# Channel-major images and residual, contexts formed from x itself, probabilities normalised on GpSimd, and values held stationary in the last product

## The chip, the cores and the metric

The kernel runs on one core of one Trainium2 chip. The metric is device microseconds (us) of one execution; each version is run several times and compared by its median. A core has a matrix engine (PE, TensorE; its weight loads are listed apart as PEld), a vector engine (DVE), a scalar engine (ACT), a general one (POOL, GpSimd), and a sync engine (SP) which in this kernel issues all data transfers (DMA). Matrix products are written into PSUM, from which DVE and ACT take them into SBUF.

## The reference

The input x is 16 images of 64 x 64 pixels with 256 channels, all in f32. Two layers follow one another, each as x = x + layer(group_norm(x)), where the norm has 32 groups of 8 channels and averages over the image. Cut to what matters:

```python
def layer0(x):                       # linear attention, 8 heads of 32
    q, k, v = split(x @ w_qkv)       # each (b, head, 32, 4096 tokens)
    q = softmax(q, over the 32 features) * SCALE
    k = softmax(k, over the 4096 tokens)
    context = einsum('bhdn,bhen->bhde', k, v)
    out = einsum('bhde,bhdn->bhen', context, q)
    return out @ w_out

def layer1(x):                       # local attention, 8 heads of 32, 7 x 7 window
    q, k, v = x @ Wq + bq, x @ Wk + bk, x @ Wv + bv
    kp = unfold(k, 7) + e            # 49 keys a query; e: embedding of row or column offset
    attn = softmax(einsum('bhwnd,bhwndk->bhwnk', q, kp))
    return einsum('bhwndk,bhwnk->bhwnd', unfold(v, 7), attn)

x = x + layer0(group_norm(x))
x = x + layer1(group_norm(x))
```

## The kernel before

Sixteen images are worked on one after the other. An image lies in 8 strips (`NS`) of 8 rows, 512 tokens each. The host hands x over in blocks of 8 x 8 pixels, and a strip in SBUF is a tile `xs` of 128 partitions by four times 256 channels: tokens lie on the partitions, two blocks to a column of tokens, four such columns (`t`) to a strip. The `xs` tiles are the residual: both layers add into them, and they are stored from there.

**Layer 0** (`layer0`, from L257) has these stages.

- The head. Every strip is transposed on PE (tile `xt`, 8 transposes a strip, L265) and evacuated by `evac`, which alternates between ACT (L80) and DVE (L82), into `xT`: channels on the partitions, 4096 tokens along them, two halves of 128 channels. `bn_stats` (L269) gathers the statistics. `group_norm` averages them over the groups with two small products (`pm`, L239, and `pv`), takes the reciprocal root on GpSimd (L251) and normalises `xT` in place, 8 operations of 128 x 1024 on DVE (L255).
- Keys. For two groups (`hg`) of four heads and 8 strips, `pk` (L280) is copied by ACT to `kT`, whose row maximum and exponentials over the tokens follow; `rz` is the reciprocal of their sum, times SCALE.
- Contexts. For each group and strip, four transposes of `kT` and eight value products (both in `pkv`, L313 and L317) are evacuated, and four products of 128 columns add to `pc` (L327) over all strips. The four heads' diagonal blocks go to `ctx_bd` (L336), which times w_out gives `pw` (L338) and, scaled by `rz`, `w2` (L339).
- Query strips. `queries` (L348 to L366) makes `pq`, its maximum, difference (L360), exponentials, sums and reciprocals, and a multiplication on GpSimd (L366) gives `qs`. `outputs` transposes `qs` (`pqt`, L373), evacuates it to `qT`, forms `py` (L383: a slice of `qT` stationary, `w2` moving in 256 columns) and adds it to `xs` (L391). `transposed` transposes the sum back to channel-major rows in `xT` (tile `xt` again, L398) with new `bn_stats`. The loop runs queries(s), outputs(s-1), transposed(s-2). The second norm follows.

**Layer 1** begins with `values` (`pv`, L424), whose strips have a bias added and are written to a padded image `vpad` in DRAM. Then for each of two head groups:

- `queries_keys`: `pka` (L454), whose four heads are copied with bias into the padded key tiles `kaug` (ACT L467, DVE L469); then 16 rounds in which GpSimd writes position columns into the query weights (`wqa`, L472, and `comb`, L477) and PE makes queries (`pqa`, L487), which DVE adds into `qa` (L504). In the second group the columns read for a round are 16 apart.
- `local_attention`: each strip has four steps (`t`), a step being two blocks of 64 queries and four heads. `load_window` (L445) fetches the values of a strip's windows, 14 x 14 keys a block, in 14 DMAs one strip ahead, into two buffers (`win`). In `scores`, 8 products (L519) of 196 columns make `s`; DVE takes the negative maxima `nm` (L528); ACT makes four exponentials of 128 x 196 (`p`, L539), and each gives its row sum in `z`. In `weighted`, 8 transposes of `p` (`pt`, L554) are evacuated into `pT`, and 16 products (L560) add to `o`: 64 queries on the partitions by 32 features in the columns, with a slice of `pT` stationary (64 columns) and values moving (32 columns); the two blocks `j` lie in the two halves of the partitions. `finish` takes the reciprocal of 16 sums (L571), multiplies `o` by it into `on` (L573) on DVE, and GpSimd adds `on` to `xs` (L580). In the second group `done` follows: the strip is stored (L602), and when a strip is stored, the previous strip's tile is loaded with the next image (L227).

As written, `weighted` of a step comes after `scores` of the next. A scheduler then orders the instructions of each engine by its own estimate: from the third strip of a group on, PE has the 16 products `o` of four steps together, in one batch a strip.

The buffers: `xs` 8; `work` 6 tiles of 128 x 1024 (p, pT, on, kv, qs, qT, v4 share them); `small` 2 by default; PSUM three pools of 2: `ps2` (s, pq, pkv, pqt, py, xt, pv: two banks each), `ps1` (pk, pka, pqa, pt), `pso` (o, pc, pw and the norm's sums).

Of the kernel before, what the change touches and what calls it, by code (L numbers as in the profile page):

```python
# [10 lines left out]
F32 = mybir.dt.float32  # L11
# [7 lines left out]
W = 64  # L19
C = 256  # L20
HEADS, HD = 8, 32
NS = 8  # strips of 8 image rows
# [3 lines left out]
WIN = 8 + 2 * PAD  # rows and columns of keys that an 8x8 block of queries sees  # L26
NCH = WIN // 2 * WIN  # keys of half a window
# [4 lines left out]
# Columns of the packed constants.  # L32
# [4 lines left out]
def shape_constants():  # L37
    """What depends on shapes alone: group averaging, band selectors and masks."""
# [24 lines left out]
def attention_kernel(ctx: ExitStack, tc: tile.TileContext, x, w_qkv, w_out, wq, bq, wk, bk, wv, bv, emb0, emb1, cpk, onehot, out):  # L63
    nc = tc.nc
    B = x.shape[0]
# [48 lines left out]
    # Keys with their position one-hot: 32 rows of a head, 16 for the row and 16 for the  # L114
    # column (both modulo 16), two heads to a tile. Borders stay zero keys.
# [6 lines left out]
    # Query weights with columns for the positional scores of the current residue.  # L122
# [12 lines left out]
    with tc.tile_pool(name="setup", bufs=1) as sp:  # L135
# [27 lines left out]
        for hg in range(2):  # L163
# [16 lines left out]
            # Scores of a query against the embeddings, as columns of the query weights.  # L180
# [14 lines left out]
            # The same of the query bias, by residue, with the band's mask.  # L195
# [26 lines left out]
    work = ctx.enter_context(tc.tile_pool(name="work", bufs=6))  # L222
    small = ctx.enter_context(tc.tile_pool(name="small", bufs=2))

    def load_strip(b, s):
        t = xp.tile([P, 4, C], F32, tag="xs", name=f"xs{b}_{s}")
        nc.sync.dma_start(t.rearrange("p t c -> p (t c)"), x[b, s])  # L227
        return t

    def group_norm(xT, stats, eps, name):  # L230
        """xT normalised in place, by groups of 8 channels over the image."""
# [20 lines left out]
        for q in range(4):  # L252
            for k in range(2):
                sl = xT[:, k, q * 1024 : (q + 1) * 1024]
                nc.vector.tensor_scalar(sl, sl, mean[:, k : k + 1], rstd[:, k : k + 1], ALU.subtract, ALU.mult)  # L255

    def layer0(b, xs):  # L257
        """x += linear attention of its normalised self; returns the transposed result, normalised."""
        xT = cp.tile([P, 2, NT], F32, tag="xT", name=f"xT{b}")
        st = small.tile([P, 2, NS, 6], F32, tag="st", name=f"st0_{b}")  # L260
        for s in range(NS):
            pt = psum2(f"xt0_{b}_{s}")
            for t in range(4):
                for k in range(2):
                    nc.tensor.transpose(pt[:, k, t * P : (t + 1) * P], xs[s][:, t, k * P : (k + 1) * P], ident)  # L265
            for k in range(2):
                dst = xT[:, k, s * 512 : (s + 1) * 512]
                evac(dst, pt[:, k])
                nc.vector.bn_stats(st[:, k, s], dst)  # L269
        group_norm(xT, st, 1e-5, f"0_{b}")  # L270

        # Keys, exponentiated over the tokens.
        kT, rz = [], []
        for hg in range(2):
            kt = big.tile([P, NT], F32, tag="qk", name=f"kT{b}_{hg}")
            km = small.tile([P, NS], F32, tag="km", name=f"km{b}_{hg}")
            for s in range(NS):
                pk = psum1(f"pk{b}_{hg}_{s}")
                for k in range(2):
                    nc.tensor.matmul(  # L280
                        pk,
                        wqkv_sb[:, k, C + hg * P : C + (hg + 1) * P],
                        xT[:, k, s * 512 : (s + 1) * 512],
                        start=(k == 0),
                        stop=(k == 1),
                    )
# [13 lines left out]
            nc.vector.tensor_scalar(r, r, SCALE, None, ALU.mult)  # L300
# [3 lines left out]
        # Contexts by head, taken through the output weights.  # L304
        w2 = cp.tile([P, 2, C], F32, tag="w2", name=f"w2_{b}")
        for hg in range(2):
            pc = psum_o(f"pc{b}_{hg}")
            for s in range(NS):
                kv = work_tile(f"kv{b}_{hg}_{s}")
                pkv = psum2(f"pkv{b}_{hg}_{s}")  # L310
                for t in range(4):
                    tok = slice(s * 512 + t * P, s * 512 + (t + 1) * P)
                    nc.tensor.transpose(pkv[:, 0, t * P : (t + 1) * P], kT[hg][:, tok], ident)  # L313
                for t in range(4):
                    tok = slice(s * 512 + t * P, s * 512 + (t + 1) * P)
                    for k in range(2):
                        nc.tensor.matmul(  # L317
                            pkv[:, 1, t * P : (t + 1) * P],
                            xT[:, k, tok],
                            wqkv_sb[:, k, 2 * C + hg * P : 2 * C + (hg + 1) * P],  # L320
                            start=(k == 0),
                            stop=(k == 1),
                        )
                evac(kv[:, :512], pkv[:, 0])
                evac(kv[:, 512:], pkv[:, 1])
                for t in range(4):
                    nc.tensor.matmul(  # L327
                        pc[:, :P],
                        kv[:, 512 + t * P : 512 + (t + 1) * P],
                        kv[:, t * P : (t + 1) * P],  # L330
                        start=(s == 0 and t == 0),
                        stop=(s == NS - 1 and t == 3),
                    )
            for h in range(4):
                sl = slice(h * HD, (h + 1) * HD)
                nc.vector.tensor_copy(ctx_bd[hg][sl, sl], pc[sl, sl])  # L336
            pw = psum_o(f"pw{b}_{hg}")
            nc.tensor.matmul(pw[:, :C], ctx_bd[hg], wout_sb[:, hg], start=True, stop=True)  # L338
            nc.vector.tensor_scalar(w2[:, hg], pw[:, :C], rz[hg], None, ALU.mult)  # L339
# [3 lines left out]
        def queries(s):  # L343
            """Softmax of a strip's queries over each head's features, transposed."""
            pq = psum2(f"pq{b}_{s}").rearrange("p a (t c) -> p (a t) c", c=C)
            for t in range(4):
                for k in range(2):
                    nc.tensor.matmul(  # L348
                        pq[:, t],
                        xT[:, k, s * 512 + t * P : s * 512 + (t + 1) * P],  # L350
# [18 lines left out]
        def outputs(s, qs):  # L369
            pt = psum2(f"pqt{b}_{s}")  # L370
            for t in range(4):
                for hg in range(2):
# [7 lines left out]
            py4 = py.rearrange("p a (t c) -> p (a t) c", c=C)  # L380
            for t in range(4):
                for hg in range(2):
                    nc.tensor.matmul(  # L383
                        py4[:, t],
                        qT[:, hg * 512 + t * P : hg * 512 + (t + 1) * P],
                        w2[:, hg],
# [3 lines left out]
            flat = xs[s].rearrange("p t c -> p (t c)")  # L390
            nc.vector.tensor_tensor(flat, py.rearrange("p a c -> p (a c)"), flat, ALU.add)  # L391

        def transposed(s):
            """The strip's sum, transposed from blocks of 8x8 to rows."""
            pt = psum2(f"xt1_{b}_{s}")
            for t in range(4):
                for k in range(2):
                    nc.tensor.transpose(pt[:, k, t * P : (t + 1) * P], xs[s][:, t, k * P : (k + 1) * P], ident)  # L398
            for k in range(2):
                dst = xT[:, k, s * 512 : (s + 1) * 512]  # L400
                evac(
                    dst.rearrange("p (r c w) -> p c r w", r=8, c=8),
                    pt[:, k].rearrange("p (c r w) -> p c r w", r=8, c=8),
                )
                nc.vector.bn_stats(st[:, k, s], dst)

        held = {}
        for s in range(NS + 2):
            if s < NS:
                held[s] = queries(s)  # L410
            if 0 < s <= NS:
                outputs(s - 1, held.pop(s - 1))
            if s > 1:
                transposed(s - 2)
        group_norm(xT, st, 1e-5, f"1_{b}")
        return xT
# [235 lines left out]
```

## Time and profile before

| | |
|---|---|
| time, median of 3 runs | 10178.1 us (10175.57 to 10181.25) |
| span of the profiled execution | 10159.9 us |
| one image of it (16 in a row) | 635 us |
| PE busy | 8906.7 us, 88% |
| PEld busy | 6291.8 us, 62% |
| DVE busy | 4871.0 us, 48% |
| ACT busy | 3437.7 us, 34% |
| POOL busy | 964.1 us, 9% |
| DMA, share of 16 engines, hardware queue | 13.7% |

How to read the profile: a row of it names a source line (L554 is line 554 of the kernel before), an engine, an operation, output <- inputs, the size of one instruction and how often it ran; then busy us in all, mean ns of one, and the idle us of the engine just before such instructions, with what ended most of it ("<-DVE pT" is a DVE operation on tile `pT`). On PE a product in f32 has two instructions, so that counts are twice those in the code. A row of the timeline begins with the time of its start and its length, both in us; `x16` is the number of instructions in it, and the bracket behind it the idle time before it and what ended that. Transposes count as MATMUL with `ident`. PE's ends are modelled, so that starts are surer than lengths. The granted clock of PE is a share of its full rate; in the page's 40 slices it stands at 0.9 or more.

### The profile page before, as it was taken

To read this page: it belongs to the slowest core of one execution; us is meant where nothing else is said; L and a number is where in the kernel's file an instruction comes from. 1 tells how busy PE (TensorE), PEld (TensorE's weight loads), DVE (VectorE), ACT (ScalarE), POOL (GpSimd) and SP (SyncE) were. 2 spreads that over 40 slices of the span, in tenths; PEclk is the share of its full clock that TensorE was granted. 3 is DMA by queue.
4 is the path that set the end of the run, shared out by engine and by line. 5 is a ranking of instruction groups with operands and counts; after the bars stand their busy time and mean duration, and the time that the engine had idled before them with its cause. 6 is when DMAs were issued, how large, how long until landed. Compare 5 with 4: busy or idle time off the path is not lost. (4 is left out here: it accounts for less than half of the span.)

```text
span 10159.9 us, 193328 instructions
## 1 busy us (share of the span) xinstructions
PE 8906.7 (88%) x80084; PEld 6291.8 (62%) x80084; DVE 4871.0 (48%) x7126; ACT 3437.7 (34%) x11009; POOL 964.1 (9%) x1461
## 2 busy tenths in 40 slices
PE   7988989889898898988989889898898988989888
PEld 5666566665666656666565665656656566565665
DVE  4445454454544545445454454544545445444454
ACT  2332423324233242342423424234242342413434
POOL 1101001010010100101001010010100101001010
PEclk9999999999899999999999999999999999999999
DMA  1111101111011110111101111011110111101111
GB/s 43 49 54 31 53 19 49 54 33 53 18 49 54 33 53 18 49 54 33 55 18 47 54 33 59 21 40 54 35 58 20 38 54 36 60 22 34 54 38 48
DMA packets 562853, 425.97 MB, mean 42 GB/s; under 512 B 59548, under 2 KB 528156, under 8 KB 561856
## 3 DMA queue, kind: packets, MB, share of 16 engines
q1 hardware_dynamic: 561984, 413.61, 13.7%
q8 instruction: 640, 10.49, 0.4%
q14 instruction: 229, 1.88, 0.1%
HBM read 277.51 MB, written 135.86 MB: 41 GB/s over the span
## 5 line engine op out<-in xcount | busy, mean ns | idle before, releaser
L539 ACT ACTIVATE p<-s,nm 128x196 f32<-128x196 f32 x4096 | 1679.1, 423 | 2602.2 <-DVE nm L528 2345.5
L554 PE MATMUL pt<-ident,p 128*98 128x128 f32 x8192 | 1455.2, 305 | 319.4 <-DVE pT L82 236.5
L554 PEld LDWEIGHTS pt<-ident,p 128*98 128x98 f32 x8192 | 913.6, 139 | 892.8 <-issue 411.6
L519 PE MATMUL s<-kaug,qa 64*64 64x196 f32 x16384 | 1417.3, 371 | 3.8 <-DVE qa L504 3.8
L487 PE MATMUL pqa<-xT,wqa 128*128 128x256 f32 x4096 | 1353.6, 496 | 44.3 <-DVE qa L504 25.7
L528 DVE TENSOR_REDUCE nm<-s 128x4 f32<-128x784 f32 x1024 | 994.2, 974 | 474.9 <-PE s L519 440.3
L82 DVE COPY pT<-pt 98x512 f32<-98x512 f32 x1024 | 706.1, 690 | 1006.9 <-PE pt L554 961.0
L487 PEld LDWEIGHTS pqa<-xT,wqa 128*128 128x128 f32 x4096 | 783.2, 200 | 613.0 <-issue 415.2
L560 PEld LDWEIGHTS o<-vw,pT 98*64 98x64 f32 x32768 | 1018.7, 138 | 168.3 <-issue 140.7
L560 PE MATMUL o<-vw,pT 98*64 98x32 f32 x32768 | 1094.0, 224 | 7.5 <-ACT pT L80 5.1
L519 PEld LDWEIGHTS s<-kaug,qa 64*64 64x64 f32 x16384 | 691.9, 142 | 411.8 <-issue 323.3
L504 DVE TENSOR_TENSOR qa<-pqa,comb 128x256 f32<-128x256 f32 x1024 | 544.5, 532 | 831.0 <-PE pqa L487 830.5
L539 ACT ACTIVATION_READ_ACCUMULATOR p<-s,nm 128x1 f32 x4096 | 837.7, 205 | 0.0
L383 PE MATMUL py<-w,qT 128*128 128x256 f32 x2048 | 578.4, 443 | 200.0 <-DVE qs L360 172.2
L80 ACT COPY pT<-pt 98x512 f32<-98x512 f32 x1024 | 607.9, 594 | 339.3 <-PE pt L554 305.7
L580 POOL TENSOR_TENSOR xs<-xs,on 128x512 f32<-128x512 f32 x256 | 324.3, 1267 | 4040.4 <-DVE on L573 4040.4
L467 ACT ACTIVATE kaug<-pka,bk_sb 32x512 f32<-32x512 f32 x512 | 351.1, 686 | 1039.6 <-DVE kaug L469 1030.0
L383 PEld LDWEIGHTS py<-w,qT 128*128 128x128 f32 x2048 | 432.4, 221 | 327.7 <-issue 188.2
L454 PE MATMUL pka<-xT,wk_sb 128*128 128x512 f32 x1024 | 497.1, 616 | 118.9 <-ACT kaug L467 118.9
L317 PE MATMUL pkv<-wqkv_sb,xT 128*128 128x128 f32 x4096 | 538.8, 277 | 0.0
L469 DVE TENSOR_SCALAR kaug<-pka,bk_sb 32x512 f32<-32x512 f32 x512 | 379.7, 742 | 284.2 <-ACT kaug L467 180.8
L280 PE MATMUL pk<-xT,wqkv_sb 128*128 128x512 f32 x1024 | 485.1, 635 | 34.1 <-DVE xT L255 30.1
(93 smaller groups left out, 8240.5 us busy)
## 6 DMA issues: line engine op xcount, KB each, us to landing
vw<-vpad SPq DMA_DIRECT2D x3584, 56.0 KB
xs<-in_x SPq DMA_DIRECT2D x128, 512.0 KB
vpad<-v SPq DMA_DIRECT2D x256, 256.0 KB
out<-xs SPq DMA_DIRECT2D x128, 512.0 KB
kaug<-in_shape_onehot SPq DMA_DIRECT2D x4, 612.5 KB
vpad<-zero SPq DMA_DIRECT2D x4, 210.0 KB
wqkv_sb<-in_L_conv_w_qkv SPq DMA_DIRECT2D x1, 768.0 KB
vpad<-zero SPq DMA_DIRECT2D x4, 192.0 KB
```

The lines of the kernel that those rows point to most:

```text
L80: nc.scalar.copy(dst, src)
L82: nc.vector.tensor_copy(dst, src)
L317: nc.tensor.matmul(pkv[:, 1, t * P : (t + 1) * P], xT[:, k, tok], wqkv_sb[:, k, 2 * C + hg * P : 2 * C + (hg + 1) * P], start=(k == 0), st ...
L383: nc.tensor.matmul(py4[:, t], qT[:, hg * 512 + t * P : hg * 512 + (t + 1) * P], w2[:, hg], start=(hg == 0), stop=(hg == 1),)
L454: nc.tensor.matmul(pk, wk_sb[:, k, hg * P : (hg + 1) * P], xT[:, k, s * 512 : (s + 1) * 512], start=(k == 0), stop=(k == 1),)
L487: nc.tensor.matmul(half, wa[:, k, 2 * pl : 2 * pl + 2].rearrange("p a b -> p (a b)"), rows[k][:, r::RING, :] if hg == 0 else rows[k][:, :, ...
L504: nc.vector.tensor_tensor(dst, src, add, ALU.add)
L519: nc.tensor.matmul(ps[64 * j : 64 * j + 64, ab, pl * 2 * NCH : (pl + 1) * 2 * NCH], qa[pl][rows, 8 * s + bc], kaug[pl][rows, 8 * s : 8 * s ...
L528: nc.vector.tensor_reduce(nm, s4, AX.X, ALU.max, negate=True)
L539: nc.scalar.activation(pr[:, h * 2 * NCH : (h + 1) * 2 * NCH], s4[:, ab, pl], AF.Exp, bias=nm[:, ab, pl : pl + 1], accum_out=z[:, t, h : h ...
L554: nc.tensor.transpose(pt[:NCH, h * P : (h + 1) * P], pr[:, n0 : n0 + NCH], ident)
L560: nc.tensor.matmul(o[64 * j : 64 * j + 64, t * P + h * HD : t * P + (h + 1) * HD], pT[:NCH, c * 512 + h * P + 64 * j : c * 512 + h * P + 6 ...
```

## The change

- **Layout.** The host gives x twice: channel-major (`xc`: 128 channels by 2 by 4096 tokens, in row order) and token-major (`xt`). A strip `xs` is now 128 channels by 2 by 512 tokens, and so are the residual and the output; the host transposes the result back.
- **Head and norm.** No transposes: `bn_stats` reads `xs`. The norm writes a separate tile `xn` from `xs` (16 operations of 128 x 512), and returns mean and reciprocal root.
- **Contexts.** The product of the exponentiated keys is formed with x itself, token by channel, 256 columns wide, in place of the values. The token-major halves of a strip are loaded for it (pool `tok`, two buffers of a half-strip). The sum is then scaled by `rz`, the mean subtracted, transposed, scaled by the reciprocal root and multiplied by the value weights. This is a serial sequence between the last context and `w2`; SCALE goes into `w2`.
- **Query strips.** `py` has `w2` stationary and `qT` moving in 512 columns, and comes out channel-major; it is added to `xs` and gets its `bn_stats` there. `transposed` is gone. The second norm goes into `xn1`.
- **Probabilities.** In every step a reciprocal of the four row sums follows the exponentials, and GpSimd multiplies each head's 128 x 196 of `p` by it, in place, before the transposes.
- **Last product.** A slice of the values is stationary (32 columns) and a slice of `pT` moves (64 columns); the four heads lie in four quarters of `o`'s partitions. `finish` is one DVE addition of `o` to `xs`, the columns reordered from blocks to rows.
- **Buffers.** `work` has 5 tiles for 6.

The diff, without comments, the host's side and renamed arguments (xT to xn in products):

```diff
     def load_strip(b, s):
-        t = xp.tile([P, 4, C], F32, tag="xs", name=f"xs{b}_{s}")
-        nc.sync.dma_start(t.rearrange("p t c -> p (t c)"), x[b, s])
+        t = xp.tile([P, 2, 512], F32, tag="xs", name=f"xs{b}_{s}")
+        nc.sync.dma_start(t, xc[b, :, :, s * 512 : (s + 1) * 512])
...
     def group_norm(xs, xn, stats, eps, name):
...
-        for q in range(4):
-            for k in range(2):
-                sl = xT[:, k, q * 1024 : (q + 1) * 1024]
-                nc.vector.tensor_scalar(sl, sl, mean[:, k : k + 1], rstd[:, k : k + 1], ALU.subtract, ALU.mult)
+        for s in range(NS):
+            for k in range(2):
+                nc.vector.tensor_scalar(xn[:, k, s * 512 : (s + 1) * 512], xs[s][:, k],
+                    mean[:, k : k + 1], rstd[:, k : k + 1], ALU.subtract, ALU.mult)
+        return mean, rstd
...
     def layer0(b, xs):
         for s in range(NS):
-            pt = psum2(f"xt0_{b}_{s}")
-            ...
             for k in range(2):
-                evac(dst, pt[:, k])
-                nc.vector.bn_stats(st[:, k, s], dst)
+                nc.vector.bn_stats(st[:, k, s], xs[s][:, k])
+        mean, rstd = group_norm(xs, xn, st, 1e-5, f"0_{b}")
+        pmu = psum_o(f"pmu{b}")
+        for k in range(2):
+            nc.tensor.transpose(pmu[:, k * P : (k + 1) * P], mean[:, k : k + 1].to_broadcast([P, P]), ident)
+        mu = small.tile([P, C], F32, tag="mu", bufs=1, name=f"mu{b}")
+        nc.vector.tensor_copy(mu, pmu[:, :C])
...
-            nc.vector.tensor_scalar(r, r, SCALE, None, ALU.mult)
...
+        pc = [psum_o(f"pc{b}_{hg}") for hg in range(2)]
+        for s in range(NS):
+            xtok = []
+            for i in range(2):
+                xtok.append(tok.tile([P, 2, C], F32, tag="xtok", name=f"xtok{b}_{s}_{i}"))
+                nc.sync.dma_start(xtok[i].rearrange("p t c -> p (t c)"), xt[b, s, :, i * 2 * C : (i + 1) * 2 * C])
+            for hg in range(2):
+                ptk = psum1(f"ptk{b}_{s}_{hg}")
+                for t in range(4):
+                    nc.tensor.transpose(ptk[:, t * P : (t + 1) * P], kT[hg][:, s * 512 + t * P : s * 512 + (t + 1) * P], ident)
+                ek = work_tile(f"ek{b}_{s}_{hg}")[:, :512]
+                evac(ek, ptk)
+                for t in range(4):
+                    nc.tensor.matmul(pc[hg][:, :C], ek[:, t * P : (t + 1) * P], xtok[t // 2][:, t % 2],
+                        start=(s == 0 and t == 0), stop=(s == NS - 1 and t == 3))
+        cc = work_tile(f"cc{b}")[:, : 2 * C].rearrange("p (a c) -> p a c", c=C)
+        pct = psum1(f"pct{b}")
+        for hg in range(2):
+            nc.vector.scalar_tensor_tensor(cc[:, hg], pc[hg][:, :C], rz[hg], mu, ALU.mult, ALU.subtract)
+            for k in range(2):
+                nc.tensor.transpose(pct[:, (2 * k + hg) * P : (2 * k + hg + 1) * P], cc[:, hg, k * P : (k + 1) * P], ident)
+        cT = work_tile(f"cT{b}")[:, :512].rearrange("p (a c) -> p a c", c=P)
+        for k in range(2):
+            dst = cT[:, 2 * k : 2 * k + 2].rearrange("p a b -> p (a b)")
+            nc.vector.tensor_scalar(dst, pct[:, k * C : (k + 1) * C], rstd[:, k : k + 1], None, ALU.mult)
         for hg in range(2):
-            ...
+            px = psum_o(f"px{b}_{hg}")
+            for k in range(2):
+                nc.tensor.matmul(px[:, :P], wqkv_sb[:, k, 2 * C + hg * P : 2 * C + (hg + 1) * P], cT[:, 2 * k + hg], ...)
-                nc.vector.tensor_copy(ctx_bd[hg][sl, sl], pc[sl, sl])
+                nc.vector.tensor_copy(ctx_bd[hg][sl, sl], px[sl, sl])
...
-            nc.vector.tensor_scalar(w2[:, hg], pw[:, :C], rz[hg], None, ALU.mult)
+            nc.vector.tensor_scalar(w2[:, hg], pw[:, :C], SCALE, None, ALU.mult)
...
         def outputs(s, qs):
...
-            for t in range(4):
+            for co in range(2):
                 for hg in range(2):
                     nc.tensor.matmul(
-                        py4[:, t],
-                        qT[:, hg * 512 + t * P : hg * 512 + (t + 1) * P],
-                        w2[:, hg],
+                        py[:, co],
+                        w2[:, hg, co * P : (co + 1) * P],
+                        qT[:, hg * 512 : (hg + 1) * 512],
...
-            nc.vector.tensor_tensor(flat, py.rearrange("p a c -> p (a c)"), flat, ALU.add)
+            nc.vector.tensor_tensor(xs[s], py, xs[s], ALU.add)
+            for k in range(2):
+                nc.vector.bn_stats(st[:, k, s], xs[s][:, k])
-        def transposed(s):
-            ...
...
     def local_attention(b, hg, qa, xs, done):
         def scores(s, t):
...
+            r = small.tile([P, 4], F32, tag="rzz", bufs=3, name=f"rz{b}_{hg}_{s}_{t}")
+            nc.vector.reciprocal(r, z)
+            for h in range(4):
+                sl = pr[:, h * 2 * NCH : (h + 1) * 2 * NCH]
+                nc.gpsimd.tensor_scalar(sl, sl, r[:, h : h + 1], None, ALU.mult)
...
         def weighted(s, t, pr):
...
-            for h in range(4):
+            for j in range(2):
                 for c in range(2):
-                    for j in range(2):
+                    for h in range(4):
                         nc.tensor.matmul(
-                            o[64 * j : 64 * j + 64, t * P + h * HD : t * P + (h + 1) * HD],
+                            o[h * HD : (h + 1) * HD, t * P + 64 * j : t * P + 64 * j + 64],
+                            vw[s][:, c, 2 * t + j, h * HD : (h + 1) * HD],
                             pT[:NCH, c * 512 + h * P + 64 * j : c * 512 + h * P + 64 * j + 64],
-                            vw[s][:, c, 2 * t + j, h * HD : (h + 1) * HD],
...
         def finish(s):
-            z, o = state.pop(s)
-            ...
-            nc.gpsimd.tensor_tensor(dst, dst, on.rearrange("p (t c) -> p t c", t=4), ALU.add)
+            o = state.pop(s)
+            dst = xs[s][:, hg].rearrange("p (r c w) -> p c r w", r=8, c=8)
+            nc.vector.tensor_tensor(dst, o.rearrange("p (c r w) -> p c r w", c=8, r=8), dst, ALU.add)
             done(s)
```

## The prediction

> **What bounds the kernel now.** I read the page's head, then the PE timeline of one image in the middle of the run (5107 to 5735 us), because 16 images pass one after the other and PE holds the order of the work.
>
> ```profile
> span 10159.9 us, 193328 instructions
> PE 8906.7 (88%) x80084; PEld 6291.8 (62%) x80084; DVE 4871.0 (48%) x7126; ACT 3437.7 (34%) x11009; POOL 964.1 (9%) x1461
> L554 PE MATMUL pt<-ident,p 128*98 128x128 f32 x8192 | 1455.2, 305 | 319.4 <-DVE pT L82 236.5
> L560 PE MATMUL o<-vw,pT 98*64 98x32 f32 x32768 | 1094.0, 224 | 7.5 <-ACT pT L80 5.1
> ```
>
> One image takes 10159.9 / 16 = 635 us. PE's 88% does not say that PE is at its peak: its ends are modelled. In layer 0 the waits stand between its groups:
>
> ```profile
> 5107.32 1.97 PE L265 MATMUL xt<-ident,xs 128*128 128x128 f32 x16
> 5115.03 3.85 PE L265 MATMUL xt<-ident,xs 128*128 128x128 f32 x16 [5.75 <-DMA xs<-in_x]
> 5122.31 0.59 PE L239 MATMUL pm<-gn,grp 128*128 128x2 f32 x2 [3.44 <-DVE gn L237]
> 5126.21 19.50 PE L280 MATMUL pk<-xT,wqkv_sb 128*128 128x512 f32 x40 [1.88 <-DVE xT L255]
> 5226.92 1.97 PE L373 MATMUL pqt<-ident,qs 128*128 128x128 f32 x8 [5.96 <-POOL qs L366]
> 5241.02 3.79 PE L383 MATMUL py<-w,qT 128*128 128x256 f32 x16 [1.79 <-DVE qs L360]
> 5244.65 1.04 PE L398 MATMUL xt<-ident,xs 128*128 128x128 f32 x8
> 5246.13 3.72 PE L348 MATMUL pq<-wqkv_sb,xT 128*128 128x256 f32 x16 [0.44 <-DVE xs L391]
> ```
>
> The reader sees the image's head (18.9 us from the last `o` to the first `pk`), and the loop over query strips. In the attention the same strip of four steps repeats:
>
> ```profile
> 5069.03 3.81 PE L560 MATMUL o<-vw,pT 98*64 98x32 f32 x124
> 5074.32 0.61 PE L554 MATMUL pt<-ident,p 128*98 128x128 f32 x4 [1.48 <-DVE pT L82]
> 5075.97 1.58 PE L519 MATMUL s<-kaug,qa 64*64 64x196 f32 x14
> 5079.31 0.91 PE L519 MATMUL s<-kaug,qa 64*64 64x196 f32 x16
> 5086.01 3.81 PE L560 MATMUL o<-vw,pT 98*64 98x32 f32 x124
> ```
>
> `o` of a whole strip is done in one batch, and batch to batch is 16.98 us (5069.03 to 5086.01). Of 14 `s` in 1.58 us and 16 in 0.91 us the first ran at a granted clock of 0.5: after each idle stretch PE is slow for some us. The first two strips of a head group run step by step, 3.12 us each (`o` x32 at 5415.57 and 5418.69).
>
> **Layer 0, part by part.** Head: the transposes of x go, and with them, behind the last load, 3.85 us (16 at low clock) and an evacuation (0.67); the residual add of GpSimd (L580, 1.27 us) in front of the store and the reload goes too. The loads, bn_stats and the norm's chain stay: -5.8 us.
>
> Contexts: from the end of `pk` (5159.5) to the first `py` (5229.6) are 70.1 us. After: 64 transposes of kT at 0.109 us (4 take 0.43) = 7.0; 64 matmuls of 256 columns, each two instructions at 0.216 (`pq`, 16 in 3.45) = 27.6 in place of the value products and narrower contexts; two `pq` groups = 6.9, as before. In the built order they stand among the `pk` and the contexts, so the 5.96 us wait for `qs` goes. New is a serial tail: two scalar_tensor_tensor, transposes, scaling, `px`, four block copies (0.187 each), `pw`, `w2` (0.48), twice in part: some 7 us of such rows and 15 hand-overs of about 0.2 = 10. Then `pqt` and its evacuation, 2.7. The xtok loads have two half-strip buffers: a half is in use for 2.6 of a strip's 4.3 us of PE; a load of 256 KB costs about 2 us (half the bytes of xs, which issues in 0.38 and moves in 1.7), so 4.6 a strip: +2.4. Sum 56.6: -13.5 us.
>
> Queries: the transposes back (1.04) and the 0.44 us wait go out of each of 8 rounds, the `py` columns stay (4 x 512 for 8 x 256); 8 x 1.45 = 11.6, and the norm reads xs where it lies. -11.6 us. Normalising is 16 x 0.54 for 8 x 0.807 us on DVE, behind `pk` and `pv`: 0; uncovered it is +2 a norm.
>
> Layer 0: -30.9 us an image.
>
> **The last product.** Now 128 instructions a strip at 30.7 ns (124 in 3.81 us), two column halves at a time: 61 ns a pair. After, four quarters, each with 32 stationary and 64 moving columns. No row shows this form. `s` has four tiles in turn: 16 of 196 columns in 0.91 us, where one at a time (0.216 / 256 a column) would be 2.65, so four do run together. Lower end: 61 ns for four, 1.96 us a strip, -1.97. Upper end: one at a time, 64 columns at 54 ns, 6.9 us, +3.0. I take the lower end, nearest to `s`.
>
> The Trainium skill, TensorEngine Tiling (Array Packing), Instruction Overhead, gives each matmul about 60 cycles whatever its width and warns against tiling a small dimension; by that (25 ns at its clock) 128 would be an estimated 3.2 us and the gain 0.7. The trace's single starts inside `o` lie 6 to 7 ns apart in a pair and 58 ns from pair to pair, which speaks against a floor per instruction.
>
> **GpSimd's multiplies.** New on every step: reciprocal of 4 (about 0.2), then four 128x196 multiplies, and `pt` waits for all. Nothing else is queued on GpSimd there, but PE's later `s`, and so DVE's `nm` and ACT's exponentials, stand behind `pt`. The nearest rows:
>
> ```profile
> L472 POOL COPY wqa<-wext 128x128 f32<-128x128 f32 x512 | 148.3, 290 | 1834.7 <-PE pqa L487 1825.5 <-DVE wext L191 6.8 <-POOL comb L477 1.6
> L477 POOL TENSOR_TENSOR comb<-stat,rowc 128x128 f32<-128x128 f32 x512 | 205.1, 401 | 155.8 <-DVE qa L504 152.6 <-DVE wext L191 3.2
> L366 POOL TENSOR_TENSOR qs<-qs,qr 128x1024 f32<-128x1024 f32 x128 | 244.7, 1912 | 2664.2 <-issue 1663.5 <-DVE qr L365 1000.7
> L174 POOL MEMSET wqa<- 128x512 f32 x4 | 1.9, 522 | 0.0
> ```
>
> Lower end, as MEMSET (0.098 + 196 x 0.83 ns): 0.26 us. Upper end, as the two-input multiply (0.401 + 68 x 1.69 ns): 0.52. I take 0.36, one input like COPY (0.290 + 68 x 1 ns). A quad is 4 x 0.36 + 0.18 start = 1.6 us; 1.2 to 2.25.
>
> GPSIMD Engine Reference (Performance versus the Vector engine, Engine selection) speaks against the change: elementwise work belongs on VectorE, though one-input work is near line rate. Its 1.03 to 1.8 cycles an element at 1.2 GHz give 196 elements an estimated 0.17 to 0.29 us before dispatch, and by these the attention would end below its old time.
>
> **A strip after.** The built order still batches `o`, and work has 5 buffers for 6, so an exponential waits for an earlier pT or p. From one batch to the next, released by each other: first third of `o` 1.2; exp(2) 4 x 0.41 + 0.1 = 1.74; reciprocal 0.3; quad 1.6; pt(2) 1.2; pT copy and reciprocal 0.9; quad 1.6; pt(3) 0.9; rest of `s` 0.8; `nm` 1.0; reciprocal 0.2; quad 1.6; pt 0.8; exp 1.75; `s` 1.55. Sum 17.1, +0.1 on 17.0. In the first two strips two steps close a loop: exp 1.74, reciprocal 0.3, quad 1.6, pt 1.2, s 0.7, nm 1.1, hand-overs 0.2, o 0.5 = 7.3 for 6.24: +0.55 a step. An image: 12 x 0.1 + 16 x 0.55 = +10 us.
>
> The reciprocal and add for `on` (0.25 + 0.69 a strip) become four reciprocals and one add on DVE, 48% busy: in the chain where named, else 0; uncovered, 256 x 0.4 = 100 us. `out` and xs move in 2 KB runs for 4 KB, 14% DMA share: 0.
>
> Sum: 16 x (-30.9 + 10) = -334; 10159.9 - 334 = 9826, and the median stands 18.2 above the span: **9845 us**, -3.3%.
>
> **Rivals.** (1) *GpSimd becomes the bound of the attention, slower.* 12 x 3 + 16 / 2 = 44 quads an image stand in the chain, 704 in all. At 2.25 us: 704 x 0.65 = +458: 10303 us. It decides from 1.6 + 334 / 704 = 2.07 us a quad, 0.47 us a multiply. For it: every two-input row; against: one tensor input, plain runs. (2) *The xtok loads set the contexts' pace.* If a load is as late as xs at the head (5.75, a store and a load): 8 x (2.6 + 5.75) = 66.8 for 37: +30 an image, 10323 us. Against: 14% DMA share. (3) *The new `o` is no faster* (the quarters take turns): 12 x 0.6 to 2.0 and 16 x 0.25, some 20 us an image: 10165 us, no change. (4) *A multiply costs the lower end:* 704 x -0.37 = -260: 9585 us.
>
> **How the numbers follow.** Forecast 0.55, (4) 0.10, (1) 0.21, (2) 0.08, (3) 0.06. Range 9560 to 10330: from (4) to (2), the two ends of the quad; the forecast's own range, half the quad's spread each way, is 9700 to 10080. A difference under 0.2% can't be told from none in this kernel. Faster 0.65, same 0.06, slower 0.29.
>
> **What would show it.** L555: 0.36 us a multiply, 0.47 or more for (1); `pt` idle <-POOL p. Batch to batch near 17.1 us, first strips near 3.65 a step. `o` x124 in about 1.9 us; 3.8 for (3). `pc` in strips of 4.6 us, idle <-DMA xtok small; head near 13 us. Wrong if strips pass 19 us, or layer 0 saves under 20 us.

## The result, and the profile after

| | us, median | ratio to before, 95% interval |
|---|---|---|
| before | 10179.67 (10175.57 to 10186.35) | 1 |
| after | 11578.14 (11572.0 to 11581.25) | 1.1366, 1.1349 to 1.1382 |

The change made the kernel 13.7% slower, where 3.3% faster was forecast and the range ended at 10330 us. The page of the changed kernel, its head and its costliest groups (busy us in all, mean ns of one, then the idle us before them):

```profile
span 11575.1 us, 185499 instructions
PE 9192.6 (79%) x73140; PEld 5628.5 (49%) x73140; DVE 4752.5 (41%) x7814; ACT 3267.2 (28%) x10625; POOL 3739.6 (32%) x5301
PEclk9778787787877879778787787978878778797787
L555 POOL TENSOR_SCALAR p<-p,rz 128x196 f32<-128x196 f32 x4096 | 3097.9, 775 | 2744.3 <-DVE rz L552 2744.3
L564 PE MATMUL pt<-ident,p 128*98 128x128 f32 x8192 | 2029.9, 362 | 1305.3 <-POOL p L555 1288.9
L544 ACT ACTIVATE p<-s,nm 128x196 f32<-128x196 f32 x4096 | 1683.0, 425 | 3402.3 <-DVE nm L536 2309.8
L527 PE MATMUL s<-kaug,qa 64*64 64x196 f32 x16384 | 1733.5, 466 | 194.6 <-ACT p L544 190.8
L570 PE MATMUL o<-pT,vw 98*32 98x64 f32 x32768 | 914.5, 292 | 0.8 <-issue 0.5
```

The scores and the exponentials before, by form, and the exponentials after with all their waits:

```profile
L519 PE MATMUL s<-kaug,qa 64*64 64x196 f32 x16384 | 1417.3, 371 | 3.8 <-DVE qa L504 3.8
L539 ACT ACTIVATE p<-s,nm 128x196 f32<-128x196 f32 x4096 | 1679.1, 423 | 2602.2 <-DVE nm L528 2345.5 <-PE pt L554 206.1 <-PE o L560 44.6
```

```profile
L544 ACT ACTIVATE p<-s,nm 128x196 f32<-128x196 f32 x4096 | 1683.0, 425 | 3402.3 <-DVE nm L536 2309.8 <-PE pt L564 757.2 <-DVE rz L552 244.3
```

POOL went from 964 to 3740 us busy, 3098 of it in the new multiplications: 775 ns each where the forecast had 360. The transposes `pt` now wait 1289 us for them. PE's clock, 0.9 and more before, stands at 0.7 to 0.8 in most slices (mean 0.809 for 0.930), and the same `s` cost 466 ns each where they cost 371.

Where the time went is best seen by stage. For the table below the starts and ends of PE's groups were taken image by image and averaged over images 4 to 14. Layer 0 runs from the last `o` of an image to the first `pv`, "v, k, q" from there to the first `s`, the attention from there to the last `o`, with the second head group's keys and queries in it. "Strip" is the mean distance of two batches of `o` (to about 0.1 us, by where a batch is taken to begin), "first step" that of the first `o` of two steps in a group's first two strips. The kernels below after are the experiments'.

| us an image | layer 0 | v, k, q | attention | all | strip | first step |
|---|---|---|---|---|---|---|
| before | 217.0 | 78.4 | 337.3 | 632.7 | 18.02 | 3.20 |
| after | 188.2 | 77.5 | 455.4 | 721.2 | 24.37 | 5.67 |
| e_onett | 186.9 | 77.4 | 350.7 | 615.0 | 17.88 | 3.81 |
| e_dvett | 185.8 | 77.2 | 317.6 | 580.7 | 15.85 | 3.64 |
| e_nomult | 186.1 | 77.2 | 283.8 | 547.2 | 13.82 | 2.84 |
| e_nomult6 | 177.6 | 78.0 | 308.1 | 563.7 | 14.14 | 3.22 |
| e_w33 | 177.8 | 77.8 | 419.3 | 674.9 | 18.74 | 5.74 |
| b_33 | 217.7 | 80.0 | 310.6 | 608.2 | 13.53 | 3.44 |
| b_on | 216.7 | 79.5 | 332.8 | 629.0 | 18.07 | 3.18 |
| e_mix5 | 187.6 | 77.6 | 335.6 | 600.8 | 17.21 | 3.47 |
| e_mix6 | 177.6 | 77.9 | 312.3 | 567.8 | 13.72 | 3.49 |
| v_turn | 179.9 | 77.7 | 302.4 | 560.0 | 13.41 | 3.31 |
| v_turn5 | 186.9 | 77.3 | 299.0 | 563.2 | 14.83 | 3.22 |

Layer 0 gained 28.8 us an image, close to the forecast's 30.9. The attention grew by 118.1 where +10 was forecast. That is practically all of the miss: 16 x 108 = 1730 us, where 1733 lie between 9845 and 11578.

One strip of the attention after, on all engines (start, length, engine, line, operation; in the bracket the idle time before it and what ended it):

```profile
5763.67 3.43 PE L570 MATMUL o<-pT,vw 98*32 98x64 f32 x120
...
5768.04 3.03 POOL L555 TENSOR_SCALAR p<-p,rz 128x196 f32<-128x196 f32 x4 [3.81 <-DVE rz L552]
...
5771.12 0.75 PE L564 MATMUL pt<-ident,p 128*98 128x128 f32 x5 [0.43 <-POOL p L555]
...
5771.98 0.69 DVE L82 COPY pT<-pt 98x512 f32<-98x512 f32 x1 [3.12 <-PE pt L564]
...
5772.59 0.17 DVE L552 RECIPROCAL rz<-z 128x4 f32<-128x4 f32 x1
...
5772.92 3.03 POOL L555 TENSOR_SCALAR p<-p,rz 128x196 f32<-128x196 f32 x4 [1.86 <-DVE rz L552]
...
5777.61 0.97 DVE L536 TENSOR_REDUCE nm<-s 128x4 f32<-128x784 f32 x1
5778.50 0.17 DVE L552 RECIPROCAL rz<-z 128x4 f32<-128x4 f32 x1
5778.76 3.03 POOL L555 TENSOR_SCALAR p<-p,rz 128x196 f32<-128x196 f32 x4 [2.81 <-DVE rz L552]
...
5781.85 1.09 PE L564 MATMUL pt<-ident,p 128*98 128x128 f32 x4 [0.30 <-POOL p L555]
...
5783.02 0.42 ACT L544 ACTIVATE p<-s,nm 128x196 f32<-128x196 f32 x1 [5.58 <-PE pt L564]
...
5787.52 3.43 PE L570 MATMUL o<-pT,vw 98*32 98x64 f32 x120
```

The batch starts at 5763.67 and the next at 5787.52. Three quads of 3.03 us stand between them one behind the other: each has to end before the last `pt` of its step, and the next quad waits for a reciprocal that stands in DVE's queue behind a copy of `pT` (at 5772.59) or `nm` (at 5778.50). The line at 5783.02 is the work buffers: ACT was idle for 5.58 us until a transposition set a buffer free, and over the whole run it waited 757 us in this way, 206 before.

### The profile page after: what moved, and what is told of

Same layout as the page of the kernel before. It is cut to its first block, busy times and chain, and to the rows that moved or that the text cites. A ratio compares the mean times of both kernels' runs of the same rounds, so it can differ in the third digit from the quotient of the medians.

```text
span 11575.1 us, 185499 instructions
## 1 busy us (share of the span) xinstructions
PE 9192.6 (79%) x73140; PEld 5628.5 (49%) x73140; DVE 4752.5 (41%) x7814; ACT 3267.2 (28%) x10625; POOL 3739.6 (32%) x5301
## 3 DMA queue, kind: packets, MB, share of 16 engines
q1 hardware_dynamic: 631616, 480.73, 13.8%
## 5 line engine op out<-in xcount | busy, mean ns | idle before, releaser
L555 POOL TENSOR_SCALAR p<-p,rz 128x196 f32<-128x196 f32 x4096 | 3097.9, 775 | 2744.3 <-DVE rz L552 2744.3
L564 PE MATMUL pt<-ident,p 128*98 128x128 f32 x8192 | 2029.9, 362 | 1305.3 <-POOL p L555 1288.9
L495 PE MATMUL pqa<-xn,wqa 128*128 128x256 f32 x4096 | 1356.2, 496 | 53.3 <-ACT kaug L475 31.8
L495 PEld LDWEIGHTS pqa<-xn,wqa 128*128 128x128 f32 x4096 | 793.9, 203 | 614.0 <-issue 393.2
L570 PEld LDWEIGHTS o<-pT,vw 98*32 98x32 f32 x32768 | 779.0, 157 | 338.6 <-issue 312.2
L570 PE MATMUL o<-pT,vw 98*32 98x64 f32 x32768 | 914.5, 292 | 0.8 <-issue 0.5
L405 PE MATMUL py<-qT,w 128*128 128x512 f32 x1024 | 510.1, 644 | 194.6 <-DVE qs L383 172.2
L462 PE MATMUL pka<-xn,wk_sb 128*128 128x512 f32 x1024 | 546.6, 662 | 93.9 <-ACT kaug L475 90.0
L329 PE MATMUL pc<-xtok,ek 128*128 128x256 f32 x2048 | 511.0, 400 | 82.0 <-DMA xtok<-in_xt 77.4
L290 PE MATMUL pk<-xn,wqkv_sb 128*128 128x512 f32 x1024 | 492.3, 642 | 17.7 <-DVE xn L256 17.7
```

Source lines behind the costliest of these rows:

```text
L329: nc.tensor.matmul(pc[hg][:, :C], ek[:, t * P : (t + 1) * P], xtok[t // 2][:, t % 2], start=(s == 0 and t == 0), stop=(s == NS - 1 and t = ...
L462: nc.tensor.matmul(pk, wk_sb[:, k, hg * P : (hg + 1) * P], xT[:, k, s * 512 : (s + 1) * 512], start=(k == 0), stop=(k == 1),)
L495: nc.tensor.matmul(half, wa[:, k, 2 * pl : 2 * pl + 2].rearrange("p a b -> p (a b)"), rows[k][:, r::RING, :] if hg == 0 else rows[k][:, :, ...
L555: nc.gpsimd.tensor_scalar(sl, sl, r[:, h : h + 1], None, ALU.mult)
L564: nc.tensor.transpose(pt[:NCH, h * P : (h + 1) * P], pr[:, n0 : n0 + NCH], ident)
L570: nc.tensor.matmul(o[h * HD : (h + 1) * HD, t * P + 64 * j : t * P + 64 * j + 64], vw[s][:, c, 2 * t + j, h * HD : (h + 1) * HD], pT[:NCH, ...
```

## The experiments

**Without the multiplications (e_nomult).**

```diff
-            nc.vector.reciprocal(r, z)
-            for h in range(4):
-                sl = pr[:, h * 2 * NCH : (h + 1) * 2 * NCH]
-                nc.gpsimd.tensor_scalar(sl, sl, r[:, h : h + 1], None, ALU.mult)
```

> The changed kernel without the reciprocal and without GpSimd's four multiplications of p; it leaves the normalisation by the row sums out, and nothing else. Theory A (the multiplications, 0.751 us from start to start, stand in the chain of every step): a strip falls from 23.85 us to what PE alone takes, 17.0 less the 0.3 that o gained, the first steps from 5.7 us to 3.1, and 16 images of 635 - 27 - 16 x 0.3 = 603 us make 9670 us (9550 to 9800). Theory B (one work buffer less keeps the exponentials waiting; idle time of ACT <-PE pt is 757 us in the changed kernel): that wait stays, 10200 us or more.

8817.79 us, ratio 0.8664 (0.8652 to 0.8676). Theory B falls in the form it had, and theory A's sum is 850 us too long: without the multiplications a strip takes 13.8 us, not the 16.7 that the old 17.0 had suggested. So the multiplications cost 171.6 us an image, and they hid a gain in the attention of 53.5 us, in a kernel that normalises nothing. A part of this gain can be seen in `o`. Windows over one batch, after, in e_nomult and before (us, then PE, PEld, DVE, ACT and POOL busy with counts, PE's granted clock, DMA's share, GB/s):

```profile
5763.67:5767.10 3.43, 3.43 (x124) 3.26 (x122) 2.77 (x4) 2.18 (x9) 0.56 (x1) 0.50 0.02 5
```

```profile
5307.66:5309.54 1.88, 1.88 (x125) 1.79 (x122) 1.57 (x2) 1.27 (x5) 0.00 (x0) 1.00 0.05 9
```

```profile
5069.03:5072.84 3.81, 3.81 (x125) 3.69 (x124) 0.97 (x1) 2.66 (x11) 0.00 (x0) 1.00 0.02 4
```

The same instructions take 3.43 us at a clock of 0.50 and 1.88 at 1.00; the old form took 3.81 at 1.00. The new product is twice as fast, as forecast, and this batch of after, read without its clock, would have said that it is hardly faster. The Trainium skill, TensorE: Matmul & The Clock Gate, Part 1, has two states of the clock, half rate after an idle window and full rate after a busy one. These rows agree with the two rates; what sets them no run here isolates.

**One operation in place of four (e_onett), and the same on DVE (e_dvett).**

```diff
-            for h in range(4):
-                sl = pr[:, h * 2 * NCH : (h + 1) * 2 * NCH]
-                nc.gpsimd.tensor_scalar(sl, sl, r[:, h : h + 1], None, ALU.mult)
+            p4 = pr[:, : 8 * NCH].rearrange("p (h n) -> p h n", h=4)
+            nc.gpsimd.tensor_tensor(p4, p4, r.unsqueeze(2).to_broadcast([P, 4, 2 * NCH]), ALU.mult)
```

> The four multiplications of a step become one GpSimd tensor_tensor of 128 x 784 with the reciprocals broadcast; same result. From L389 (128 x 1024 in 1.914 us) it should last 1.5 us, the 1.6 that the forecast gave the quad. If only the duration of the quad was mis-sized, a strip comes to 17 to 18.5 us (pt now waits for all four heads) and the time to 9850 to 10150 us; if the chain was miscounted too (a reciprocal stands behind copies on DVE, PE at half clock), 10300 to 10800 us; if the operation lasts 2.5 us or more, two-input or broadcast work is as slow as the scalar form, and the time stays above 11000 us.

9878.26 us, ratio 0.9706 (0.9693 to 0.9719). The group of the new operation in e_onett:

```profile
L554 POOL TENSOR_TENSOR p<-p,rz 128x784 f32<-128x784 f32 x1024 | 1528.3, 1493 | 2653.3 <-DVE rz L552 2103.7 <-PE s L527 427.8 <-PE pt L563 108.6
```

With 1.49 us, and some 0.1 from the reciprocal's end to its start, in place of 3.03 the kernel takes what was forecast for a quad of 1.6: 9878 for 9845 us, strips of 17.88 us for 17.1, first steps of 3.81 for 3.65, an attention of +13.4 us an image for +10. The multiplication's duration was the mis-sized term, not the place of the quads in the chain. That the sum comes so near is in part luck. The strips' mean is of 20.0 us in the first group, which also carries products of the second group's keys (`pka`), and of 15.7 in the second. The steps take 8.5 us an image more than before (8.8 forecast), the ten distances between batches 1.9 less (1.2 more forecast), and the rest, 6.8 more, lies at the groups' beginnings and ends and between the groups, which the forecast did not list.

> The same one operation on DVE instead of GpSimd; same result. By DVE's rows 128 x 512 in 0.69 and 128 x 1024 in 1.22 us it lasts 0.97 us. Theory A: chain 12.3 + 3 x 1.1 lies under PE's 17 us a strip; steps at the start 3.3 to 3.6 us; 9750 to 10000 us. Theory B, or DVE as the new bound (its nm, copies and the new 4 x 0.97 are 12 us of a strip, in one queue): 10300 us or more.

9342.53 us, ratio 0.9183 (0.917 to 0.9196). It came out 400 us under the range of theory A, whose 17 us a strip was again too long. The operation took 0.974 us as expected, and DVE did not become the bound.

**What GpSimd's forms cost (f_forms).** 24 operations on scratch tiles ahead of the first image, by the loop

```diff
+    for n in (64, 196, 512, 784):
+        nc.gpsimd.tensor_scalar(fa[:, :n], fa[:, :n], fr[:, 0:1], None, ALU.mult)
+        nc.gpsimd.tensor_scalar(fb[:, :n], fa[:, :n], fr[:, 0:1], None, ALU.mult)
+        nc.gpsimd.tensor_scalar(fa[:, :n], fa[:, :n], 0.5, None, ALU.mult)
+        nc.gpsimd.tensor_tensor(fa[:, :n], fa[:, :n], fb[:, :n], ALU.mult)
+        nc.gpsimd.tensor_tensor(fa[:, :n], fa[:, :n], fr[:, 0:1].to_broadcast([P, n]), ALU.mult)
+        nc.gpsimd.tensor_copy(fb[:, :n], fa[:, :n])
```

> The changed kernel with 24 GpSimd operations on scratch tiles ahead of the first image, DVE and PE idle beside them: widths 64, 196, 512 and 784, each as tensor_scalar by a column of a tile (in place, and into another tile), tensor_scalar by a constant, tensor_tensor of two tiles, tensor_tensor by a broadcast column, and a copy. Theory A1 (the scalar form itself is slow, so much an element): by a column 0.75 us at 196, 2.0 at 512, 3.0 at 784, in place or not; tensor_tensor 0.40, 1.0 and 1.5; copy 0.36 at 196. A2 (a start cost of each operation): 196 and 512 differ by less than 0.6 us in the scalar form. A3 (working in place): only the in-place form is slow. The constant form: slow as the column under A1 if the operation is slow, quick if it is the column's fetch.

Groups of f_forms at a width of 196 (busy us, mean ns of one):

```profile
L604 POOL TENSOR_SCALAR fa<-fa,fr 128x196 f32<-128x196 f32 x1 | 0.8, 772 | 0.1
L605 POOL TENSOR_SCALAR fb<-fa,fr 128x196 f32<-128x196 f32 x1 | 0.8, 772 | 0.1
L606 POOL TENSOR_SCALAR fa<-fa 128x196 f32<-128x196 f32 x1 | 0.7, 697 | 0.1
L607 POOL TENSOR_TENSOR fa<-fa,fb 128x196 f32<-128x196 f32 x1 | 0.6, 597 | 0.1
L608 POOL TENSOR_TENSOR fa<-fa,fr 128x196 f32<-128x196 f32 x1 | 0.5, 513 | 0.1
L609 POOL COPY fb<-fa 128x196 f32<-128x196 f32 x1 | 0.3, 347 | 0.1
```

At 64 and 784 columns they took 447 and 2242, 442 and 2242, 368 and 2167, 317 and 1839, 292 and 1492, 248 and 852 ns. Over 720 columns that is 2.5 ns an element for the scalar form, by a column or by a constant, 2.1 for two tiles, 1.7 for a broadcast column and 0.84 for a copy; what is left at no columns is about 0.28 us for the scalar form by a column, 0.21 by a constant and 0.18 to 0.19 for the others. A1 holds (in place makes no difference, and it is the operation, not the fetch of the scalar), though its 3.0 us at 784 was too long, because it had no start cost, and two tiles took 1.84 us there where it had 1.5. The scalar form, with one tensor input, is the dearest of all.

Nothing beside it made it so. The operation as the changed kernel ran it, by line (minimum, median, maximum ns):

```profile
L555 POOL TENSOR_SCALAR p<-p,rz x4096: 771/775/782, 305.8 to 11565.5; 128x196 f32<-128x196 f32 x196
```

4096 of them, DVE busy or idle, lie within 11 ns.

The Trainium skill, GPSIMD Engine Reference, Performance versus the Vector engine, gives two-input work about 2.6 cycles an element at 1.2 GHz, an estimated 2.2 ns, and the 2.1 above agree; it gives short bodies 1.03 cycles and a tight loop about 1.8, and the Engine selection section calls one-input work roughly line rate. The copy's 0.84 ns fit that, the scalar form's 2.5 do not, and the measurement decides.

**Buffers.** Why a strip without the quads takes less than before is asked of the buffers. b_33 is the kernel before and e_w33 the changed one, with two pools. Of e_w33 (b_33 had six tiles, and its `on` goes to `p_tile` too):

```diff
-    work = ctx.enter_context(tc.tile_pool(name="work", bufs=5))
+    pwork = ctx.enter_context(tc.tile_pool(name="pwork", bufs=3))
+    work = ctx.enter_context(tc.tile_pool(name="work", bufs=3))
+    def p_tile(name):
+        return pwork.tile([P, 8 * NCH], F32, tag="pw", name=name)
...
-            pr = work_tile(f"p{b}_{hg}_{s}_{t}")
+            pr = p_tile(f"p{b}_{hg}_{s}_{t}")
```

> The kernel before, unchanged but for its buffers: p and on take turns in three tiles of 784 columns, the rest in three of 1024, in place of six shared ones. e_mix6 ran the same products in strips of 13.7 us (mean), the kernel before in 18.0. Theory C (the shared rotation makes p and pT wait for each other and for on, which GpSimd frees late): strips fall to 14 to 15 us, 12 x 3.5 an image, 9400 to 9700 us. Rival D (the strip's length comes from the order of work, the residual's GpSimd addition or the loads): 10050 to 10250 us.

9765.19 us, ratio 0.9589 (0.9574 to 0.9603). Its strips fall to 13.53 us, below theory C's 14, and the time stays a little above C's range, since not all of the strips' gain stays: from the first group's last `o` to the second's first `s` it takes 74.7 us for 61.9 before (the attention as a whole is shorter by 26.7 us, not by the ten distances' 45). The traces show why. In every image from 4 to 14, 20 of the 32 instructions of the second group's keys (`pka`) ran within the first group's strips before; in b_33 all 32 come after that group's last `o`. The same holds in all five kernels with two pools (75 us; 57 to 62 in the others). So rival D's time falls, and the 17 us that the forecast took for a strip before were not what PE needs for these products; but the pools changed the order of work with the buffers, so theory C's reason, the rotation, is not shown apart from it.

> The changed kernel with its multiplications, buffers three of 784 columns (p, ek, cc, cT) and three of 1024 in place of five shared. If the quads of 3.03 us set the strip, whatever the buffers: 11350 to 11600 us. Theory B (the missing buffer): the 757 us in which ACT waits for pt go, 10700 to 11100 us.

10823.69 us, ratio 1.0627 (1.0609 to 1.0644), in the range of theory B, below "quads set it whatever the buffers". ACT's exponentials in e_w33:

```profile
L548 ACT ACTIVATE p<-s,nm 128x196 f32<-128x196 f32 x4096 | 1685.6, 428 | 2559.8 <-DVE nm L540 2176.1 <-DVE rz L556 367.9 <-POOL p L559 12.2
```

The wait for `pt` is gone, and 755 us with it: 36 us an image in the attention and 10 in layer 0. In the attention this is a net figure: 51.5 less in strips and steps, 15.4 more between the groups. So theory B, which fell in e_nomult without the multiplications, holds together with them.

> The kernel before with six shared buffers as they were, but on in a buffer of its own. If on in the rotation costs the strips their 4 us: near b_33, 9700 to 9900 us. If p and pT hinder each other: 10050 to 10250 us.

```diff
-            on = work_tile(f"on{b}_{hg}_{s}")[:, :512]
+            on = onp.tile([P, 512], F32, tag="on", name=f"on{b}_{hg}_{s}")
```

10055.89 us, ratio 0.9874 (0.9855 to 0.9894): within the second expectation. `on` in the rotation is a small part of what b_33 gained.

> e_nomult (no normalisation) with the same buffers three and three. If p and pT hinder each other in shared buffers also where no on takes its turn among them: 8500 to 8700 us for e_nomult's 8818. If it is on in the rotation that does the harm: 8760 to 8880 us.

9039.8 us, ratio 0.8879 (0.8865 to 0.8892): outside both. Here three and three buffers make the attention 24 us an image longer than five shared ones, in a kernel that has no `on`, and 15 of them lie between the groups, where again all of `pka` comes after the last `o`. The scheduler builds another order with other pools, and no rule for the number of buffers can be taken from these runs.

**The two halves of the change apart (e_mix6, e_mix5).** The changed layer 0 and layout with the old attention, whose result is transposed at the end of a strip (the end of `finish`, against the kernel before):

```diff
             nc.vector.tensor_tensor(on ..., o ..., r.unsqueeze(2).to_broadcast([P, 16, HD]), ALU.mult)
-            nc.gpsimd.tensor_tensor(dst, dst, on.rearrange("p (t c) -> p t c", t=4), ALU.add)
+            ont = psum_o(f"ont{b}_{hg}_{s}")
+            for t in range(4):
+                nc.tensor.transpose(ont[:, t * P : (t + 1) * P], on[:, t * P : (t + 1) * P], ident)
+            nc.vector.tensor_tensor(dst, ont.rearrange("p (c r w) -> p c r w", c=8, r=8), dst, ALU.add)
```

> The changed layer 0, layout and loads with the last product and the normalisation of the kernel before (queries on the partitions, the sums' reciprocals applied to o), then four transposes a strip of the result and one addition to xs on DVE; p, on, ek, cc, cT in three buffers of 784 columns, the rest in three of 1024. Layer 0's saving of 27 us an image stays, 16 strips pay 4 x 0.11 of PE and one DVE operation of 0.69 off the path: 635 - 27 + 16 x 0.45 = 615 us an image, 9860 us (9760 to 9980): faster than both. If the transposes hold up o or pt behind DVE's queue, +1 us a strip, 10020 us.

9128.47 us, ratio 0.8971 (0.8959 to 0.8983), 630 us under the range: it had been reckoned from the old strip.

> e_mix6 with the five shared buffers of the changed kernel. Theory C: strips go back to 16 to 18 us, 9500 to 9900 us. Rival D: 9050 to 9250 us.

9645.31 us, ratio 0.9474 (0.9458 to 0.949), theory C. With five shared buffers the attention is that of the kernel before (335.6 for 337.3 us), and what remains is the layer 0 of the change, by itself worth 5.3%.

**A version that keeps both gains (v_turn, v_turn5).** `p` stays as it is, `o` is normalised in `finish`, with buffers three and three in v_turn and five in v_turn5. The new part of v_turn's `finish`; the reciprocals and multiplications of every step are gone:

```diff
+            rb = p_tile(f"rb{b}_{hg}_{s}")[:, :512]
+            nc.gpsimd.tensor_copy(rb.rearrange("p (a d) -> p a d", d=HD), r.unsqueeze(2).to_broadcast([P, 16, HD]))
+            rt = psum1(f"rt{b}_{hg}_{s}")
+            for t in range(4):
+                nc.tensor.transpose(rt[:, t * P : (t + 1) * P], rb[:, t * P : (t + 1) * P], ident)
+            rs = p_tile(f"rs{b}_{hg}_{s}")[:, :512]
+            nc.scalar.copy(rs, rt)
+            nc.vector.tensor_tensor(rs, o, rs, ALU.mult)
...
+            nc.gpsimd.tensor_tensor(dst, rs.rearrange("p (c r w) -> p c r w", c=8, r=8), dst, ALU.add)
```

> The changed kernel with p left as it is: in finish GpSimd spreads the 16 reciprocals of a strip over 32 columns each, four transposes turn them, ACT copies them, DVE multiplies o by them and GpSimd adds to xs; buffers three and three as in e_mix6. All of the result is computed. If o's four quarters are worth their 1.9 us a strip here too, e_nomult's 8818 us plus 16 strips x 0.45 us of PE an image: 8930 us (8850 to 9050). If the transposes wait for GpSimd (0.65 us) and PE falls to half clock, 9100 to 9300 us, no better than e_mix6.

8992.38 us (8986.14 to 8999.99), ratio 0.8833 (0.882 to 0.8846), within the first range: 11.7% faster than before, and the best of all kernels that compute the whole result.

> v_turn with the five shared buffers of the changed kernel, and the spread and the turned reciprocals in the two half-strip tiles that hold x by tokens in layer 0, so that only p and pT take turns in the attention. e_nomult's attention (two head groups and the queries between) took 284 us an image with five shared buffers, e_nomult6's 308 with three and three, v_turn's 302. If that difference is the buffers' order and carries over: 284 + 7 for an attention, contexts 8 us longer, in sum 8870 us (8800 to 8950). If the turned reciprocals upset the rotation as on did in e_mix5: 9200 us or more.

9040.75 us, ratio 0.8877 (0.8863 to 0.8891), between its two cases: the attention is 3 us an image shorter than v_turn's, not 11, and layer 0 gives 7 back. The two place the same work differently. v_turn5 has 24 of the 32 `pka` in the first group's strips, which take 16.1 us where its second group's take 13.6, and 59.6 us between the groups; v_turn has none there, strips of 13.4 us in both groups, and 75.1 us between them.

## Why the prediction was wrong

- **The step that failed** is the price of a multiplication: "I take 0.36, one input like COPY", with an upper end of 0.52 from the two-input multiply. It measured 0.775 us, 0.751 from start to start. The scalar form was put between a copy and a two-input operation because it has one tensor input; f_forms shows that it is dearer than both at every width. The prediction put too much weight on counting inputs and had no row of this form; its upper end should have been left open or set well beyond the nearest row.
- **The place of the quad held.** With an operation of 1.49 us (e_onett) the kernel takes 9878 us for the forecast's 9845. That the quad stands three times in a strip's chain is thereby borne out, though not each hand-over, and the nearness of the whole is in part luck, as its parts above show. Over e_nomult the 1.49 us cost 66.9 us an image, 45 times their length, where 44 quads were counted.
- **Rival 1 named the mechanism**, GpSimd as the bound, and its place. Its own formula with the measured quad, 3.03 + 0.1 for the start, gives 9845 + 704 x 1.53 = 10920 us; its price of 2.25 gave 10303.
- **The remaining 660 us.** 16 x 36 = 580 of them go with three and three buffers in place of five (e_w33), and with them ACT's wait for a buffer. The prediction named this wait ("an exponential waits for an earlier pT or p") and gave it no price: with a short quad it is shorter (491 us of ACT's idle time in e_onett, 193 in e_nomult, for 757). The multiplications cost 171.6 us an image with five buffers and 111.2 with three and three (e_w33 less e_nomult6), so some 60 us of their price depend on the pools. How much of it is the wait, and how much the other order that the pools bring, no run separates. What is left, about 80 us, was not taken apart; PE's clock (0.79 over the strip shown, 1.00 over one of e_nomult) may have a share in it.
- **The last product.** The lower end that was taken, 1.96 us a strip, is right at full clock (120 instructions in 1.88 us). Rival 3 falls, though in the profile after the batch took 3.43.
- **Layer 0.** Head -4.3 us for -5.8, contexts -8.4 for -13.5, queries with the second norm -16.2 for -11.6, in sum -28.8 for -30.9. The loads of x by tokens (rival 2) ended 77.4 us of PE's idle time in all, 4.8 us an image, twice the forecast's 2.4. e_w33 shows 9 us an image more to be had from the contexts with buffers of their own.
- **The base of 17 us a strip** was read from one strip (the mean is 18.0) and taken as the work that must be done. b_33 does the same products in 13.53 us. This hardly moved the forecast, as far as e_onett shows, but three kernels (e_nomult, e_dvett, e_mix6) came out 400 to 730 us below the ranges expected of them on this base.

## What to carry to other kernels

Price an operation by its own form, or measure it alone ahead of the program: two neighbours do not bound it, and a term that stands 704 times in the chain must not rest on an analogy. Read a duration on PE together with its granted clock before calling a new form no faster. Where a profile shows short waits for buffers, a slower producer can lengthen them too, so that a new operation in such a loop costs more than its own time. When pools are changed, look where the scheduler put the neighbouring stage's work: what strips gained here was in part lost between the groups.

## What the runs showed of the hardware that was not expected

- GpSimd's multiplication by a scalar, 128 partitions in f32: 2.5 ns an element, for a column as for a constant, in place or not, and 0.28 us to start (0.21 for a constant); a tensor_tensor with a broadcast column does the same in 1.7 ns and 0.19 us. Four scalar forms of 196 columns took 3.03 us, one broadcast form of 784 took 1.49.
- Four matmuls in four quarters of the output's partitions, 32 stationary and 64 moving columns, at full clock: 120 instructions in 1.88 us, 15.7 ns each; two halves of 64 stationary and 32 moving columns: 124 in 3.81 us, 30.7 ns each.
- Of the order of work rather than the hardware: the same instructions with other pools made the kernel before 4.1% faster (b_33), and a kernel without the normalisation 2.5% slower (e_nomult6 against e_nomult).
